# Expert rows fetched four tiles ahead, and the first tile's scatter targets made inside the attention

## The chip, the cores and the metric

The kernel runs on one core of a Trainium2 chip. The metric is the device time of one launch in microseconds (us), the median of several runs. The engines are called as in the profile: PE (matrix products), PEld (its weight loads), DVE (vector), ACT (scalar functions), POOL (general purpose, issues indirect DMAs) and SP (issues the plain DMAs). A "q" behind an engine's name means its instruction queue, so SPq is where SP's DMAs are issued.

## The reference, cut to what matters

A 64 x 64 image of 256 channels passes four residual layers; the change concerns the last step of the last one, a mixture of experts over N = 4096 tokens with 8 experts, of which each token takes its two best:

```python
def _L3_ffn_ref(x, Wg, bg, W1, b1, W2, b2):
    xf = x.reshape(-1, D)
    gate_logits = xf @ Wg + bg
    top_w, top_i = jax.lax.top_k(gate_logits, TOP_K)
    top_w = jax.nn.softmax(top_w, axis=-1)
    w_dense = jnp.sum(jax.nn.one_hot(top_i, E, dtype=xf.dtype) * top_w[..., None], axis=1)
    out = jnp.zeros_like(xf)
    for e in range(E):
        h = jax.nn.gelu(xf @ W1[e] + b1[e], approximate=False)
        out = out + w_dense[:, e:e + 1] * (h @ W2[e] + b2[e])
    return out.reshape(B, L, D)
# ...
t = t + _L3_attn_ref(_ln_t(t), ...)   # full attention over all 4096 tokens
t = t + _L3_ffn_ref(_ln_t(t), ...)    # D = 256, hidden 1024, E = 8, TOP_K = 2
```

## The kernel before, in words

Lines are those of the kernel before, as the profile names them.

**Routing.** A token is not run through all experts. `route_parts` handles a block of 512 tokens (NBLK = 8 blocks, TPB = 4 groups of 128 tokens each): it normalises the tokens, finds the two best experts and their weights, works out for each token a row in a table `xs` in HBM where the rows of one expert stand together, and scatters the normalised tokens there with indirect DMAs from POOL (L2117, 8 a block, 1 us of POOL each). A row carries C + 4 = 260 numbers: the token, its own number, its two weights and its first expert.

**Tiles.** The table is worked off in tiles of MT = 256 rows. `full_table` makes the list of the first FULL = 20 tiles (called A, with `exA`, `inA`, `offA`) when seven of the eight blocks are routed: those tiles are full already and do not depend on the last block. `tile_table` makes the list of the rest (B) after the last block. 36 tiles run; three more stand in a conditional part that was not executed.

**The expert loop** (`expert_tiles`) works on tile i in these steps:
- `load` (`expert_load`, L2219) has SP read two table entries into registers and issue three DMAs: the rows f_x (L2229, 260 KB), the first weights f_w1 (L2231, 1028 KB) and the second weights f_w2 (L2233, 1152 KB). It runs `ahead` = 2 tiles before the tile is used. The rows have ahead + 3 = 5 buffers; each of the two weights has two, and every third tile uses a third one, lent from the pool `keep`. So SP waits before f_w2 until the tile three before has been finished with.
- `turn` (`expert_turn`, L2238) transposes the rows on PE (L2241); DVE copies them out as f_xT (L2242).
- `first` forms f_h_ps = f_w1 x f_xT, eight groups of 128 hidden units (PE, L152) in three PSUM buffers; ACT takes them out with the gelu (L2303).
- `where` (L2320 to L2333) works out, from f_x and the tables, where each row's output goes (f_at) and its weight (f_wgt): nine DVE operations on 128 x 2 numbers. The first, f_first (L2325), needs the rows of f_x; f_at (L2331) is what the output's scatter reads its targets from. Each result has four buffers, so f_at of tile k takes the place of that of tile k - 4 and waits until the scatter of tile k - 4 has ended.
- `sides` has POOL form four differences of the second weights (f_wt, L2344).
- `second` with `seven` (L2347 on) forms the product with f_w2 in seven instead of eight parts: DVE makes four sums of f_h (f_hs, L2351 to L2354), PE the products f_ya and f_yb, ACT a copy (L2368), DVE the sums (L2369 to L2373) and the bias add, called Y in the text (f_y, L2379). ACT scales Y by the token's weight (L2386), and POOL scatters it in two halves to the table `ys` (L2387).

The loop issues for tile i: load(i + 2), first(i), sides(i), a step of the last block's routing, turn(i + 1), where(i + 1), second(i - 1), a further step. So the second product lags one tile.

**Around the start.** The attention of this layer (`attn3`, L2485 on) goes over 8 blocks of queries and, in each, over 16 pairs of key groups. While it computes its last block, it routes the block before last, then builds table A and loads tile 0 (at pair j = TPB + 5 = 9) and turns its rows (at j = NPAIR - 2 = 14) into f_xT. The last block's attention output is finished (`finish`: PE a_q_ps, DVE f_r L2707 and t L2708) between the parts of tile 0's first product, and its routing is spread over the first tiles as six `steps`: the scatters of its rows to xs fall in tile 2's iteration, tile_table in tile 3's.

**What sets the order.** PE's and POOL's order in the attention, and PE's in the expert loop until the six steps are done, is the order in which the code is written. DVE's, ACT's and SP's order there is chosen by a scheduler from the dependences[...]. SP's row fetch for a tile waits for all scatters to xs that were issued before it in the program.

Of the kernel before, what the change touches and what calls it, by code (L numbers as in the profile page):

```python
# [10 lines left out]
F32 = mybir.dt.float32  # L11
BF16 = mybir.dt.bfloat16
I32 = mybir.dt.int32
# [6 lines left out]
P = 128  # L20
C = 256
# [71 lines left out]
class Net:  # L93
# [30 lines left out]
    def weights(self, pool, names):  # L124

        for i, name in enumerate(names):
            src = self.A[name].rearrange("(k p) n -> p k n", p=P)
            w = pool.tile(list(src.shape), F32, tag=name, name=name)
            eng = self.nc.sync if i % 2 == 0 else self.nc.scalar
            eng.dma_start(out=w, in_=src)  # L130
            self.w[name] = w

    def rows(self, pool, first, last):

        lo, hi = PR[first].start, PR[last].stop
# [2083 lines left out]
    def expert_load(self, S, tab, j, x, w1, w2, rows_first):  # L2219
        nc, A, L = self.nc, self.A, S["L"]  # L2220
        why = "worked out from counts of tokens"
        e = nc.values_load(tab[0:1, 0, j : j + 1], engines=[mybir.EngineType.SP], min_val=0, max_val=(NE - 1) * P,
                           skip_runtime_bounds_check_because=why)
        row = nc.values_load(tab[0:1, 1, j : j + 1], engines=[mybir.EngineType.SP], min_val=0, max_val=NE * N - MT,
                             skip_runtime_bounds_check_because=why)
        src = self.xs[bass.ds(row, MT), :].rearrange("(i p) c -> p i c", p=P)
        x = x()
        if rows_first:
            nc.sync.dma_start(out=x, in_=src)  # L2229
# [3 lines left out]
        nc.sync.dma_start(out=w2, in_=A[f"f{L}_w2"][bass.ds(e, P), :])  # L2233
        if not rows_first:
            nc.sync.dma_start(out=x, in_=src)
        return x, w1, w2

    def expert_turn(self, x, p, xT):  # L2238
        for k in range(2):
# [29 lines left out]
    def expert_tiles(self, S, order, wp, ps, steps, early, pre, written):  # L2269
        nc, A = self.nc, self.A  # L2270
        L = S["L"]
        tiles = range(len(order))
        of = lambda i, nm: S[order[i][0]][nm]
# [4 lines left out]
        def load(i):  # L2278
            if pre and i == 0:
                return pre["tile"]  # L2280
# [3 lines left out]
            return self.expert_load(  # L2284
                S, of(i, "tab"), order[i][1],
                lambda: wp.tile([P, NI, CX], F32, tag="x", name="f_x", bufs=ahead + 3),
                lambda: pool.tile([P, 2 * hidden + KH], F32, tag="w1", name="f_w1", **kw),
                lambda: pool.tile([P, KH * C + C], F32, tag="w2", name="f_w2", **kw),
                i > 0,
            )  # L2290

        def turn(x):
            p = ps.tile([P, 2, MT], F32, tag="x", name="f_x_ps", bufs=1 if early else 2)
            return self.expert_turn(x, p, wp.tile([P, 2, MT], F32, tag="xT", name="f_xT", bufs=3))
# [23 lines left out]
            return h  # L2318

        def where(i, x):  # L2320

            tl = lambda tag, dt=F32: wp.tile([P, NI], dt, tag=tag, name="f_" + tag, bufs=4)
            first, second, to, wgt, at = tl("first"), tl("second"), tl("to"), tl("wgt"), tl("at", I32)
            op, j = nc.vector, order[i][1]
            op.tensor_scalar(first, x[:, :, C + 3], of(i, "ex")[:, j : j + 1], None, ALU.is_equal)  # L2325
            op.tensor_scalar(second, first, -1.0, 1.0, ALU.mult, ALU.add)
            op.tensor_tensor(wgt, second, x[:, :, C + 2], ALU.mult)
            op.tensor_scalar(second, second, float(N), None, ALU.mult)
            op.tensor_tensor(to, x[:, :, C], second, ALU.add)
            op.tensor_tensor(to, to, of(i, "in")[:, j, :], ALU.mult)  # L2330
            op.tensor_tensor(at, to, of(i, "off")[:, j, :], ALU.add)  # L2331
            op.tensor_tensor(first, first, x[:, :, C + 1], ALU.mult)
            op.tensor_tensor(wgt, wgt, first, ALU.add)  # L2333
            return at, wgt

        def sides(w2):

# [61 lines left out]
        ld = {i: load(i) for i in tiles[:ahead]}  # L2399
        if pre:  # L2400
            for f in pre["ahead"][:1]:
                f()
            xT = pre["xT"]
        else:
            xT = turn(ld[tiles[0]][0])
        to = where(tiles[0], ld[tiles[0]][0])
        done = None
        for i in tiles:
            if i + ahead <= tiles[-1]:
                ld[i + ahead] = load(i + ahead)  # L2410
            x, w1, w2 = ld.pop(i)
            h = first(xT, w1, (pre["ahead"][1:] if i == 0 else ()) if steps else None)
            now = (i, h, w2, sides(w2)) + to
            step()
            if i < tiles[-1]:
                xT = turn(ld[i + 1][0])
                to = where(i + 1, ld[i + 1][0])
            if done is not None:
                second(*done)
                step()  # L2420
            done = now
# [61 lines left out]
    def attn3(self, t, S):  # L2483
# [6 lines left out]
        with (  # L2490
# [28 lines left out]
            if True:  # L2519
# [181 lines left out]
                def finish(b, i):  # L2701
                    o = bank()[:, : C + 1]
                    at = oTs[b].rearrange("p m h n -> p m (h n)")[:, :, i * P : (i + 1) * P]
                    self.mm(o, [(at[:, kt, :], wvp[:, kt, :]) for kt in range(2)])
                    ti = b * TPB + i
                    r = S["r"][:, ti : ti + 1]
                    nc.vector.reciprocal(r, o[:, C : C + 1])  # L2707
                    nc.vector.scalar_tensor_tensor(t[:, ti, :], o[:, :C], r, t[:, ti, :], ALU.mult, ALU.add)  # L2708
# [41 lines left out]
                with tc.manual_schedule(engines={ET.PE, ET.Pool}):  # L2750
                    steps = iter(())
                    for g in range(first, G + LAG):
                        if g < G:
                            scores(g)
                        values(g - LAG)
                        if g + 3 < G:
                            fetch(g + 3)
                        b, j = divmod(g - LAG, NPAIR)
                        if b > 0:
                            if j < TPB:  # L2760
                                finish(b - 1, j)
                            elif j == TPB:
                                steps = route((b - 1) * TPB, TPB)
                            elif j % 2 == 0 or b == NBLK - 1:
                                next(steps, None)
                            if b == NBLK - 1 and j == TPB + 5:
                                self.full_table(S, keep, bank)
                                one = lambda shape, tag: keep.tile([P] + shape, F32, tag=tag, name="f_" + tag, bufs=1)
                                tile = self.expert_load(S, S["A"]["tab"], 0, lambda: one([NI, CX], "x"), lambda: one([16 * P + 8], "w1"),
                                                        lambda: one([9 * C], "w2"), True)  # L2770
# [5 lines left out]
            self.experts(  # L2776
                S, [go] * 5 + [lambda: self.tile_table(S, keep, bank, True)],
                {"pool": keep, "tile": tile, "xT": xT, "ahead": [lambda i=i: finish(NBLK - 1, i) for i in range(TPB)]},
            )

    def limits3(self, S, pool):
# [252 lines left out]
```

## Time and profile before

| what | us |
|---|---|
| median of 3 runs | 3458.88 (3456.22 to 3459.38) |
| the profiled execution | 3404.69 |
| its span, first to last instruction | 3402.80 |
| PE busy in the span | 3095.0 (91%) |
| DVE busy | 2299.0 (68%) |
| POOL busy | 1460.9 (43%) |
| granted TensorE clock, mean | 0.958 of full |

Where the stages of interest lie in that span:

| stretch of the span, us | what runs | PE busy, us |
|---|---|---|
| 2700 to 2824 | attention, last block of queries | 123.57 of 124.00 |
| 2826 to 2848 | end of the attention, tile 0 | 17.26 of 22.00 |
| 2848 to 2877.5 | tiles 1 and 2 | 29.50 of 29.50 |
| 2891.5 to 2917.5 | tile 4 | 16.09 of 26.00 |
| 2931 to 3337 | steady run of expert tiles | 400.76 of 406.00 |
| 3337 to 3402.8 | last tile, outputs | 42.82 of 65.80 |

How to read the profile's lines: a line of the timeline has the start in us, the duration in us, the engine, the line of code, the operation, out<-in by the program's names, shape, and how many equal instructions were joined (x8). In brackets at its end stands how long the engine was idle before it, and what ended the wait: "<-DMA f_x<-xs" is the landing of that transfer. A line of the waits names engine, tile and line that waited, what it waited for, then us in total, how many times, and the longest. The profiled execution is a single one, and shorter than the median of the timed runs; differences worked out on it are carried over to the median.

### The profile page before, as it was taken

How to read it: one execution, taken by the hardware profiler on the slowest of the kernel's cores; microseconds unless marked ns; L12 is line 12 of the kernel's file. 1: busy time of each engine (PE TensorE's matmuls, PEld its weight loads, DVE VectorE, ACT ScalarE, POOL GpSimd, SP SyncE). 2: the span in 40 equal slices, each digit the busy share in tenths (PEclk: the TensorE clock that was granted, in tenths of full speed). 3: DMA queues.
4: the chain of work that ended last, by engine and by line, in shares of the span. 5: the costliest groups of instructions: out<-in, count | busy, mean ns of one | idle time of the engine just before them, and what ended most of it. 6: DMA issues, size and time to landing. Idle time of an engine off the chain costs nothing.

```text
span 3402.8 us, 66193 instructions
## 1 busy us (share of the span) xinstructions
PE 3095.0 (91%) x25774; PEld 2314.3 (68%) x25774; DVE 2299.0 (68%) x5331; ACT 1329.1 (39%) x2552; POOL 1460.9 (43%) x1318
## 2 busy tenths in 40 slices
PE   6789999999977899797969789999999999899997
PEld 3343444344435888766857567888888888789996
DVE  8885677577764777787855576777777776555552
ACT  4444343434425666343633352322222223333331
POOL 2028787878842555433444353000000013555552
PEclk9889999999988999898979899999999999999998
DMA  1145555521134122200158553223332224555554
GB/s 72 42 109 147 159 153 156 155 66 52 46 107 127 57 75 75 58 1 2 54 186 262 190 212 118 90 96 100 100 99 100 81 95 165 184 201 208 203 204 176
DMA packets 241688, 407.01 MB, mean 120 GB/s; under 512 B 78353, under 2 KB 152850, under 8 KB 231890
## 3 DMA queue, kind: packets, MB, share of 16 engines
q1 hardware_dynamic: 212002, 344.40, 31.7%
q0 software_dynamic: 13056, 35.93, 2.8%
q10 hardware_dynamic: 16304, 22.31, 2.0%
q8 instruction: 207, 3.39, 0.4%
q14 instruction: 119, 0.97, 0.1%
HBM read 287.07 MB, written 111.30 MB: 117 GB/s over the span
## 4 chain that ended last, share of the span: by engine, by line
PE 41%; DVE 8%; DMA 5%; issue 4%; ACT 3%; POOL 3%; SPq 0%; POOLq 0%; DVEq 0%; ACTq 0%
PE a_sa_ps L2653 6%; PE f_h_ps L152 6%; PE a_oa_ps L2692 3%; PE a_ob_ps L2692 3%; DMA ys<-f_y,f_at 3%; PE a_oc_ps L2692 3%; PE a_sb_ps L2653 3%; PE f_ya_ps L152 3%; PE l_acc_ps L1160 2%; PE f_yb_ps L152 2%; POOL ys L2387 2%; PE a_od_ps L2692 1%; PE a_q_ps L152 1%; PE a_sc_ps L2653 1%; PE a_qkv_ps L152 1%
## 5 line engine op out<-in xcount | busy, mean ns | idle before, releaser
L776 ACT COPY l_sc<-l_s 128x384 f32<-128x384 f32 (+1 forms) x632 | 304.0, 532 | 452.3 <-PE l_s L769 446.2
L781 DVE TENSOR_TENSOR l_sm<-l_s,mask 128x256 f32<-128x256 f32 (+2 forms) x628 | 308.1, 551 | 90.4 <-PE l_s L769 89.2
L152 PE MATMUL f_h_ps<-f_xT,f_w 128*128 128x256 f32 x1440 | 342.2, 388 | 29.1 <-ACT f_h L2303 19.0
L2117 POOL DMA_INDIRECT xs<-f_room,f_to x64 | 64.3, 1005 | 641.9 <-DVE a_e L2640 474.9
L152 PEld LDWEIGHTS f_h_ps<-f_xT,f_w 128*128 128x128 f32 x1440 | 262.7, 192 | 92.3 <-ACT f_h L2303 42.2
L769 PE MATMUL l_s<-l_q,l_k 32*128 32x256 f32 (+3 forms) x2944 | 270.5, 453 | 0.0
L2672 ACT ACTIVATE a_e<-a_e 128x512 f32<-128x512 f32 x256 | 156.2, 630 | 245.2 <-DVE a_e L2642 240.9
L786 POOL TENSOR_TENSOR l_sm<-l_sc,mask 128x768 f32<-128x768 f32 (+1 forms) x116 | 202.5, 1754 | 87.8 <-ACT l_sc L776 87.7
L2303 ACT ACTIVATE f_h<-f_h_ps,f_w 128x256 f32<-128x256 f32 x360 | 164.8, 470 | 178.7 <-PE f_h_ps L152 178.5
L1156 DVE TENSOR_TENSOR l_pr<-l_vk,l_w_ps 128x1280 f32<-128x1280 f32 x128 | 186.6, 1482 | 54.2 <-PE l_acc_ps L1160 35.0
L769 PEld LDWEIGHTS l_s<-l_q,l_k 32*128 32x128 f32 x2944 | 132.4, 183 | 115.2 <-issue 67.5
L2387 POOL DMA_INDIRECT ys<-f_y,f_at x144 | 147.8, 1027 | 146.2 <-ACT f_y L2386 115.9
L1160 PE MATMUL l_acc_ps<-ident,l_pr 128*128 128x128 f32 x1600 | 197.9, 278 | 6.5 <-POOL l_pr L1151 6.2
L1160 PEld LDWEIGHTS l_acc_ps<-ident,l_pr 128*128 128x128 f32 x1600 | 184.5, 144 | 13.3 <-POOL l_pr L1151 8.2
L790 POOL TENSOR_TENSOR l_sm<-l_sc,mask 128x256 f32<-128x256 f32 (+1 forms) x220 | 185.1, 869 | 15.3 <-ACT l_sc L776 14.4
L2344 POOL TENSOR_TENSOR f_wt<-f_w 128x512 f32<-128x512 f32 x72 | 90.1, 1272 | 225.0 <-PE f_ya_ps L152 201.1
L2653 PE MATMUL a_sa_ps<-a_q,a_kt 128*128 128x256 f32 x512 | 156.2, 387 | 15.6 <-DVE a_u L2658 14.7
L2657 ACT COPY a_u<-a_sa_ps 128x256 f32<-128x256 f32 x128 | 47.6, 372 | 293.7 <-PE a_sa_ps L2653 293.6
L2653 PE MATMUL a_sa_ps<-a_qt,a_kt 128*128 128x256 f32 x512 | 153.6, 382 | 0.0
L815 PE MATMUL l_b_ps<-l_sm,l_v 128*32 128x256 f32 (+2 forms) x2176 | 153.5, 372 | 0.0
L786 POOL TENSOR_TENSOR l_sm<-l_sc,mask_c 128x768 f32<-128x768 f32 (+1 forms) x64 | 122.3, 1929 | 36.5 <-ACT l_sc L776 36.0
L2692 PE MATMUL a_ob_ps<-a_et,a_vs 128*128 128x256 f32 x512 | 132.2, 381 | 0.0
(590 smaller groups left out, 7272.4 us busy)
## 6 DMA issues: line engine op xcount, KB each, us to landing
a_kt<-a_kd SPq DMA_DIRECT2D x128, 512.0 KB
f_w<-in_f_w SPq DMA_DIRECT2D x36, 1152.0 KB
f_w<-in_f_w SPq DMA_DIRECT2D x36, 1028.0 KB
xs<-zero SPq DMA_DIRECT2D x8, 4160.0 KB
l_vk<-vt SPq DMA_DIRECT2D x180, 128.0 KB
f_x<-xs SPq DMA_DIRECT2D x72, 260.0 KB
f_w<-in_f_w SPq DMA_DIRECT2D x36, 384.0 KB
l_rcp<-l_recd SPq DMA_DIRECT2D x48, 256.0 KB
```

What stands on the lines that cost most here:

```text
L152: self.nc.tensor.matmul(out, lhsT, rhs, start=(i == 0), stop=(i == len(pairs) - 1))
L769: nc.tensor.matmul(s[pair, j][:, at : at + m, :], key(hp), qs[hp], start=(z == 0), stop=(z == len(pieces) - 1))
L776: nc.scalar.copy(sc[:, j], s[1, j])
L781: nc.vector.tensor_tensor(to(pair, j, kind, at), pick(s[pair, j], kind, which), mask, ALU.mult)
L786: nc.gpsimd.tensor_tensor(out[:, :, at, :], of[:, :, which, :], bc(mask, 1, 2), ALU.mult)
L790: nc.gpsimd.tensor_tensor(to(1, j, kind, at), pick(sc[:, j], kind, which), mask, ALU.mult)
L1156: nc.vector.tensor_tensor(pr, vk, bc(held["w"][:, j, dy], 3, D), ALU.mult)
L1160: nc.tensor.matmul(acc[:, m, j, :], pf[:, dx, m * P : (m + 1) * P], self.ident, is_transpose=True, start=(j == 0 and dy == 0 and dx == 0 a ...
L2303: nc.scalar.activation(h[:, m, :], p[:, m % 2, :], AF.Gelu, bias=w1[:, 2 * hidden + m : 2 * hidden + m + 1])
L2387: nc.gpsimd.indirect_dma_start(out=self.ys_parts[(i % 4) * NI + k], in_=y[:, k, :], in_offset=None, out_offset=bass.IndirectOffsetOnAxis(a ...
L2653: mm = lambda out, i, right: nc.tensor.matmul(out, A[i], right, start=True, stop=True)
L2692: nc.tensor.matmul(out, vs[:, j, i, :], right, start=(j == 0 and side != 1), stop=(j == NPAIR - 1 and side != 0))
```

## The change

`expert_load` is cut into `expert_at` (one table entry into a register), `expert_rows` (the rows' DMA) and `expert_weights` (the two weights' DMAs), and `where` becomes `expert_where`, so that each can be called by itself. In the loop of the last layer, the rows of tile i + 4 and the weights of tile i + 2 are now asked for in iteration i (both were i + 2); the rows have 7 buffers instead of 5. With that, the rows of tiles up to 6 are asked for ahead of the last block's scatters; it was up to tile 4. Tile 0's nine operations of `where` are now written inside the attention, at pair 14, behind the transposition of its rows, into buffers of their own. The expert loop of the layer before has the same distances as it had.

```diff
+    def expert_at(self, tab, k, j, most):
+        return self.nc.values_load(tab[0:1, k, j : j + 1], engines=[mybir.EngineType.SP], min_val=0, max_val=most,
+                                   skip_runtime_bounds_check_because="worked out from counts of tokens")
+
+    def expert_rows(self, tab, j, x):
+        row = self.expert_at(tab, 1, j, NE * N - MT)
+        self.nc.sync.dma_start(out=x, in_=self.xs[bass.ds(row, MT), :].rearrange("(i p) c -> p i c", p=P))
+        return x
+
+    def expert_weights(self, L, tab, j, w1, w2):
+        nc, A = self.nc, self.A
+        e = self.expert_at(tab, 0, j, (NE - 1) * P)
         w1 = w1()
         nc.sync.dma_start(out=w1, in_=A[f"f{L}_w1"][bass.ds(e, P), :])
         w2 = w2()
         nc.sync.dma_start(out=w2, in_=A[f"f{L}_w2"][bass.ds(e, P), :])
...
+    def expert_where(self, T, j, x, tl):
+        first, second, to, wgt, at = tl("first"), tl("second"), tl("to"), tl("wgt"), tl("at", I32)
...
         ahead = 3 if L == 2 else 2 if pre or not early else 1
+        ahead_x = ahead + 2 if pre else ahead
...
+            return self.expert_rows(*tab(i), wp.tile([P, NI, CX], F32, tag="x", name="f_x", bufs=ahead_x + 3))
...
         def where(i, x):
             tl = lambda tag, dt=F32: wp.tile([P, NI], dt, tag=tag, name="f_" + tag, bufs=4)
+            return self.expert_where(S[order[i][0]], order[i][1], x, tl)
...
-        to = where(tiles[0], ld[tiles[0]][0])
+            xT, to = pre["xT"], pre["to"]
...
         for i in tiles:
+            if i + ahead_x <= tiles[-1]:
+                xs[i + ahead_x] = rows(i + ahead_x)
             if i + ahead <= tiles[-1]:
-                ld[i + ahead] = load(i + ahead)
-            x, w1, w2 = ld.pop(i)
+                ws[i + ahead] = weights(i + ahead)
+            w1, w2 = ws.pop(i)
...
             if i < tiles[-1]:
-                xT = turn(ld[i + 1][0])
-                to = where(i + 1, ld[i + 1][0])
+                xT = turn(xs[i + 1])
+                to = where(i + 1, xs[i + 1])
...
                             if b == NBLK - 1 and j == NPAIR - 2:
-                                xT = self.expert_turn(tile[0], bank().rearrange("p (k n) -> p k n", k=2), one([2, MT], "xT"))
+                                pre["xT"] = self.expert_turn(pre["x"], bank().rearrange("p (k n) -> p k n", k=2), one([2, MT], "xT"))
+                                tl = lambda tag, dt=F32: keep.tile([P, NI], dt, tag="e" + tag, name="f_" + tag, bufs=1)
+                                pre["to"] = self.expert_where(S["A"], 0, pre["x"], tl)
```

More of the change, by code (lines that the diff above doesn't have):

```diff
@@ L2217, in tile_table @@
             nc.vector.scalar_tensor_tensor(part, self.nth[:, : k * NI], float(2 * N), part, ALU.add, ALU.mult)
[L2219 to L2229, printed above, removed]
+    def expert_at(self, tab, k, j, most):
[8 more added lines that the diff above has]
+        e = self.expert_at(tab, 0, j, (NE - 1) * P)
         w1 = w1()
@@ L2233, in expert_load @@
         nc.sync.dma_start(out=w2, in_=A[f"f{L}_w2"][bass.ds(e, P), :])
-        if not rows_first:
-            nc.sync.dma_start(out=x, in_=src)
-        return x, w1, w2
+        return w1, w2
+    def expert_where(self, T, j, x, tl):
+        first, second, to, wgt, at = tl("first"), tl("second"), tl("to"), tl("wgt"), tl("at", I32)
+        op = self.nc.vector
+        op.tensor_scalar(first, x[:, :, C + 3], T["ex"][:, j : j + 1], None, ALU.is_equal)
+        op.tensor_scalar(second, first, -1.0, 1.0, ALU.mult, ALU.add)
+        op.tensor_tensor(wgt, second, x[:, :, C + 2], ALU.mult)
+        op.tensor_scalar(second, second, float(N), None, ALU.mult)
+        op.tensor_tensor(to, x[:, :, C], second, ALU.add)
+        op.tensor_tensor(to, to, T["in"][:, j, :], ALU.mult)
+        op.tensor_tensor(at, to, T["off"][:, j, :], ALU.add)
+        op.tensor_tensor(first, first, x[:, :, C + 1], ALU.mult)
+        op.tensor_tensor(wgt, wgt, first, ALU.add)
+        return at, wgt
     def expert_turn(self, x, p, xT):
@@ L2272, in expert_tiles @@
         tiles = range(len(order))
-        of = lambda i, nm: S[order[i][0]][nm]
+        tab = lambda i: (S[order[i][0]]["tab"], order[i][1])
         hidden = 256 if L == 2 else 1024
@@ L2276, in expert_tiles, with rows, weights @@
         ahead = 3 if L == 2 else 2 if pre or not early else 1
-        def load(i):
+        ahead_x = ahead + 2 if pre else ahead
+        def rows(i):
             if pre and i == 0:
-                return pre["tile"]
+                return pre["x"]
+            return self.expert_rows(*tab(i), wp.tile([P, NI, CX], F32, tag="x", name="f_x", bufs=ahead_x + 3))
+        def weights(i):
+            if pre and i == 0:
+                return pre["w"]
             lent = pre and i % 3 == 0
@@ L2283, in load @@
             kw = dict(bufs=1) if lent else dict(bufs=2) if early else {}
-            return self.expert_load(
-                S, of(i, "tab"), order[i][1],
-                lambda: wp.tile([P, NI, CX], F32, tag="x", name="f_x", bufs=ahead + 3),
+            return self.expert_weights(
+                L, *tab(i),
                 lambda: pool.tile([P, 2 * hidden + KH], F32, tag="w1", name="f_w1", **kw),
                 lambda: pool.tile([P, KH * C + C], F32, tag="w2", name="f_w2", **kw),
-                i > 0,
             )
@@ L2322, in where @@
             tl = lambda tag, dt=F32: wp.tile([P, NI], dt, tag=tag, name="f_" + tag, bufs=4)
[L2323 to L2334, printed above, removed]
+            return self.expert_where(S[order[i][0]], order[i][1], x, tl)
         def sides(w2):
@@ L2398, in expert_tiles @@
         nc.scalar.activation(wp.tile([P, 1], F32, tag="g", name="f_gelu", bufs=1), self.one, AF.Gelu)
-        ld = {i: load(i) for i in tiles[:ahead]}
+        xs, ws = {}, {}
+        for i in tiles[:ahead_x]:
+            if pre or i > 0:
+                xs[i] = rows(i)
+            if i < ahead:
+                ws[i] = weights(i)
+            if i not in xs:
+                xs[i] = rows(i)
         if pre:
-            for f in pre["ahead"][:1]:
-                f()
-            xT = pre["xT"]
-        else:
-            xT = turn(ld[tiles[0]][0])
-        to = where(tiles[0], ld[tiles[0]][0])
+            pre["ahead"][0]()
+            xT, to = pre["xT"], pre["to"]
+        else:
+            xT = turn(xs[tiles[0]])
+            to = where(tiles[0], xs[tiles[0]])
         done = None
         for i in tiles:
+            if i + ahead_x <= tiles[-1]:
+                xs[i + ahead_x] = rows(i + ahead_x)
             if i + ahead <= tiles[-1]:
-                ld[i + ahead] = load(i + ahead)
-            x, w1, w2 = ld.pop(i)
+                ws[i + ahead] = weights(i + ahead)
+            w1, w2 = ws.pop(i)
+            xs.pop(i)
             h = first(xT, w1, (pre["ahead"][1:] if i == 0 else ()) if steps else None)
@@ L2768, in attn3 @@
                                 one = lambda shape, tag: keep.tile([P] + shape, F32, tag=tag, name="f_" + tag, bufs=1)
-                                tile = self.expert_load(S, S["A"]["tab"], 0, lambda: one([NI, CX], "x"), lambda: one([16 * P + 8], "w1"),
-                                                        lambda: one([9 * C], "w2"), True)
+                                tab = S["A"]["tab"], 0
+                                pre = {"pool": keep, "x": self.expert_rows(*tab, one([NI, CX], "x")),
+                                       "w": self.expert_weights(3, *tab, lambda: one([16 * P + 8], "w1"), lambda: one([9 * C], "w2"))}
                             if b == NBLK - 1 and j == NPAIR - 2:
-                                xT = self.expert_turn(tile[0], bank().rearrange("p (k n) -> p k n", k=2), one([2, MT], "xT"))
+                                pre["xT"] = self.expert_turn(pre["x"], bank().rearrange("p (k n) -> p k n", k=2), one([2, MT], "xT"))
+                                tl = lambda tag, dt=F32: keep.tile([P, NI], dt, tag="e" + tag, name="f_" + tag, bufs=1)
+                                pre["to"] = self.expert_where(S["A"], 0, pre["x"], tl)
             left.close()
@@ L2777, in attn3 @@
                 S, [go] * 5 + [lambda: self.tile_table(S, keep, bank, True)],
-                {"pool": keep, "tile": tile, "xT": xT, "ahead": [lambda i=i: finish(NBLK - 1, i) for i in range(TPB)]},
+                {**pre, "ahead": [lambda i=i: finish(NBLK - 1, i) for i in range(TPB)]},
             )
```

## The prediction, as put on record before the changed kernel ran

> **What bounds the kernel now.** I read the page first (shares of the engines, then the chain that ended last), then the windows of the last stage, then its waits, then the timelines of DVE, PE, POOL and SP around the stalls.
>
> ```profile
> PE 3095.0 (91%) x25774; PEld 2314.3 (68%) x25774; DVE 2299.0 (68%) x5331; ACT 1329.1 (39%) x2552; POOL 1460.9 (43%) x1318
> ...
> PE 41%; DVE 8%; DMA 5%; issue 4%; ACT 3%; POOL 3%; SPq 0%; POOLq 0%; DVEq 0%; ACTq 0%
> ```
>
> PE is the bound of the whole, so a change pays only where PE stands still. The windows of the last stage (columns: width of the window, then busy us and instructions of PE, PEld, DVE, ACT, POOL, granted clock, DMA share, GB/s):
>
> ```profile
> 2826.00:2848.00 22.00, 17.26 (x75) 14.07 (x74) 17.41 (x59) 8.08 (x14) 10.10 (x8) 0.92 0.62 240
> ...
> 2891.50:2917.50 26.00, 16.09 (x95) 14.16 (x94) 10.71 (x52) 4.63 (x11) 10.70 (x11) 0.80 0.50 177
> ...
> 2931.00:3337.00 406.00, 400.76 (x2688) 365.57 (x2688) 221.74 (x577) 140.41 (x324) 223.00 (x177) 1.00 0.53 195
> ```
>
> The long third row is the steady run of expert tiles: PE idles 5.2 of 406 us. What can be won lies in the two short rows, which hold one stall each:
>
> ```profile
> 2830.91 1.13 DVE L2326 TENSOR_SCALAR f_second<-f_first 128x2 f32<-128x2 f32 x1
> ...
> 2835.09 1.11 PE L152 MATMUL a_q_ps<-a_wvp,a_oT 128*128 128x257 f32 x4 [1.99 <-DVE t L2708]
> 2836.04 3.48 PE L152 MATMUL f_h_ps<-f_xT,f_w 128*128 128x256 f32 x8
> ```
>
> ```profile
> 2900.09 0.59 DVE L2325 TENSOR_SCALAR f_first<-f_x,f_exA 128x2 f32<-128x2 f32 x1 [10.23 <-DMA f_x<-xs]
> ...
> 2906.86 3.78 PE L152 MATMUL f_h_ps<-f_xT,f_w 128*128 128x256 f32 x8 [9.91 <-ACT f_h L2303]
> ```
>
> In the first, tile 0's nine small operations hold DVE at 2830.65, the last block's f_r and t come late, and PE waits 1.99 us. In the second, DVE stands 10.23 us before tile 5's f_first, whose rows wait for the last block's scatters; with DVE held, tile 2's output comes late, ACT's scale of it late, the gelus behind that late, and PE waits 9.91 us. In the steady run, the waits between 2931 and 3320 (us in total, times, longest) hold the pair that matters below, and SP's own wait (2826 to 3340) the third:
>
> ```profile
> DVE f_at L2331 <- DMA ys<-f_y,f_at: 35.7, 25, 2.9
> PE f_h_ps L152 <- ACT f_h L2303: 5.2, 8, 1.8
> ```
>
> ```profile
> SPq L2233 <- DVE f_y L2379: 378.3, 33, 16.1
> ```
>
> DVE already waits before f_at for the landing of an older tile's scattered output, 1.4 us each, harmlessly.
>
> **What the Trainium skill says.** "PSUM — Partial Sum Buffer", section "Engine vs sequencer instructions": the queue of VectorE is strict FIFO; the trace agrees (10.23 us held). "SBUF — State Buffer", section "Who interferes with whom": a VectorE instruction with two SBUF inputs and a GpSimd instruction that reads SBUF exclude each other; the trace agrees, since Y's bias add (L2379) takes 0.69 us alone (2904.46) and 1.24 beside f_wt on POOL (2932.32), f_hs 0.69 and 1.25. "DMA: Bandwidth & Descriptors", section "Anatomy of one DMA — SWDGE (gpsimd) path": some 2 us are fixed, mostly until the last byte is confirmed; the trace's ys scatters took 2.4 us at best, 6.5 in the median, so the rest is queueing. "TensorE: Matmul & The Clock Gate", section "What's actually happening": half clock after an idle window of about 3.4 us; here eight f_h products took 3.48 us instead of 1.89 after an idle of only 1.99, and 3.78 after 9.91, so the measurement decides.
>
> **The change, part by part.** I take the order of instructions from the changed program as built, where only SP's and DVE's orders differ in the part that runs.
>
> *1. Tile 0's nine operations leave 2830.65.* The 1.99 idle goes, and with it the half-clock stretch (3.48 − 1.89 = 1.6): −3.6 at most. What is late next is tile 1's set on the same engine and a_q's own chain; I take −2.5, bounds −3.7 and 0.
>
> *2. They go into the attention.* In the built order tile 0's f_first stands on DVE between L2641 and L2642 of a pair, which is 2808.01 on the clock of before. It reads rows that SP only issues at 2811.76 (behind block 6's scatters, which POOL issues until 2810.1). A row fetch took 2.8 us (2897.30 to 2900.09), so DVE stands from 2808.0 to 2814.5. Behind it are L2642 (0.34) and L2643 (0.68), which free the score banks at 2815.7; PE wants the next scores at 2810.97. In 2700 to 2824 PE is busy 123.57 of 124 us, so nothing hides it: a stall of 4.75, and 1.6 of half clock, together +6.4 (bounds +4 and +7, if the clock stays or the wait shortens).
>
> *3. Rows four tiles ahead.* SP's two extra fetches (260 KB each; x3 and x4, 0.9 us of SP each) go where SP waits long anyway (378 us in all): nothing; without that cover 2 × 0.9. x5 and x6 now lie ahead of the scatters. The first fetch behind them is x7, and on DVE tile 7's f_first stands where tile 5's stood, before tile 2's output. It waits for the same landing: the 10.23 moves from tile 5 to tile 7, and tile 4's 25.95 us (2891.58 to 2917.53, against 13.62) stays. Gain 0; bounds −12.3 (25.95 − 13.62, all gone) and +1. To escape, rows would have to land by 2890, before POOL has issued the scatters (2895.6).
>
> *4. The nine operations of the steady run.* Their rows being there earlier, DVE's order is another one. Before, per tile: f_hs, f_xT, f_hs, ..., f_at(i+2), then the sums of output i−1 and its bias add Y. f_at has four buffers: f_at(k) waits for the landing of scatter(k−4), here a tile and a half old. After: Y(i), five of tile i+4's operations, f_hs, **f_at(i+4)**, then f_hs, f_xT, f_hs, f_hs, the sums, Y(i+1). Now f_at(i+4) waits for scatter(i): of the output that DVE has just finished. Queued behind it are f_xT, which PE's next tile needs, and Y(i+1). That closes a loop: Y, ACT scale, two scatters on POOL, landing, f_at, the rest, next Y.
>
> Its length. From Y's end to the landing: where Y was late before, so that POOL was free of f_wt, Y ended at 2949.75 and its scatters
>
> ```profile
> 2950.57 0.99 POOL L2387 DMA_INDIRECT ys<-f_y,f_at  x1 [1.36 <-ACT f_y L2386]
> 2951.86 1.12 POOL L2387 DMA_INDIRECT ys<-f_y,f_at  x1 [0.30 <-ACT f_h L2303]
> ```
>
> landed by 2958.5: 8.7. Five late ones gave 8.4 to 9.4; the weights that the same Y releases on SP (2.4 MB) lie before them. I take 8.6. From f_at to Y's end: f_at 0.1, f_hs 0.61, f_xT 0.6, f_hs 0.6 and 0.6, small ones 0.5, sums 1.9, Y 0.69 (spacings at 2925 to 2933): 5.6 alone. POOL's four f_wt operations (2930.51 to 2936.04, 5.5 us) fall into it and stretch the three f_hs and Y by 0.55 each: 7.7 to 7.8. The loop is 8.6 + 7.7 = 16.3 (bounds 8.4 + 5.6 = 14.0 and 9.4 + 8.2 = 17.6). PE's work of a tile is 13.62, so the loop decides. Y(3) began at 2918.70 and Y(32) at 3320.96 before: 402.26 / 29 = 13.87 each, and f_at(7) to f_at(35) are 29 turns. 29 × (16.3 − 13.87) = +70.5 (bounds +4 and +108).
>
> **Sum.** +70.5 + 6.4 − 2.5 + 0 = +74.4. The profiled execution took 3404.69 us (span 3402.80 and 1.89 around it); it would become 3479.1. It lies 54.2 below the median of the runs, and I carry the difference over: 3458.88 + 74.4 = 3533.3.
>
> **Rivals.** *The loop is shorter.* If f_wt falls elsewhere or the scatters come back sooner, it is 14.0 to 15.0, say 14.5: 29 × 0.63 = +18.3, with +3.9 from the rest 3481. For it: f_wt starts when PE ends a tile's second product, and a slower tile moves that. Against: f_wt is 5.5 of 16 us and must lie somewhere. *The loop fits under PE, and the change is not slower.* Mechanism: scatters that return as fast as the best seen. Y's end to the second scatter's issue was 2949.75 to 2952.98, 3.2; with a flight of 2.4 that is 5.6, and 5.6 + 7.7 = 13.3 is under 13.62. It decides from a landing 5.9 us after Y's end. Then PE's small gaps go: 29 × (13.87 − 13.62) = −7.2, with −2.5 and +6.4 3455.6: no difference; if the wait in the attention also cost nothing, 3449.2, faster. Against: the burst of weights starts from the same Y, and no flight in the steady run was near 2.4. *The row wait goes as well* while the loop stays (the place of tile 7's f_first being harmless): −12.3, 3521; I count it within my forecast.
>
> **Chances.** Forecast (loop of 15.0 to 17.6) 0.77; short loop 0.16; loop under PE 0.07, of which 0.04 without a difference and 0.03 faster. A difference under 0.2%, 6.9 us, is what a measurement here cannot tell from none. So faster 0.03, same 0.04, slower 0.93. My forecast's own range is 29 × 1.13 + 3.9 = +37 to 29 × 3.73 + 3.9 = +112, 3496 to 3571; to leave out no more than 2 in 10 I reach into the short loop, to 3480, and leave out the rest below.
>
> **What would show it.** In the profile after: f_at behind DMA ys some 29 times, 5 to 8 us each (before at most 2.9); starts of Y 16.3 apart; PE idle before f_h behind ACT's gelu by about 2.5 us a tile; DVE 6.5 us before f_first in the attention and PE idle 4.75 after it; a wait of some 10 us before f_first still in tile 4; no PE idle near 2835. I am wrong if Y's starts lie 13.6 apart (the loop has slack), or if the row wait has gone.

## The result and the profile after

The changed kernel takes 3560.99 us (median of 6 runs, 3550.98 to 3567.60), the kernel before 3458.24 in the same comparison: a ratio of 1.0296 (95% interval 1.0279 to 1.0314), +102.8 us. Forecast were +74.4 us and 3533.3, range 3480 to 3571.

The profiled execution of the changed kernel took 3567.60 us, its span is 3565.7. That is 162.9 more than the span of before, but 55.6 of these lie ahead of the third attention, in layers that the change does not touch: the one profiled execution of before went through them faster than every later one. So stages are compared from the first score product of this attention. The views of the tile a_sa_ps give its first and last start (the two numbers ahead of the semicolon; the first fence is of before, the second of after):

```profile
L2653 PEld LDWEIGHTS a_sa_ps<-a_q,a_kt x512: 186/190/337, 1953.1 to 2819.2; 128*128 128x128 f32 x171
```

```profile
L2667 PEld LDWEIGHTS a_sa_ps<-a_q,a_kt x512: 186/190/338, 2008.7 to 2886.1; 128*128 128x128 f32 x171
```

With the starts of Y (the bias add, L2379 before, L2384 after) from the timelines of DVE, the stages are:

| stage | before, us | after, us | difference |
|---|---|---|---|
| attention, first to last a_sa | 866.1 | 877.4 | +11.3 |
| last a_sa to Y(0) | 43.95 | 45.14 | +1.2 |
| Y(0) to Y(3), with the row wait | 55.55 | 58.08 | +2.5 |
| Y(3) to Y(32), 29 turns | 402.26 (13.87 each) | 494.73 (17.06 each) | +92.5 |
| Y(32) to the end | 81.84 | 81.65 | −0.2 |
| sum | | | +107.3 |

The sum is that of the two profiled executions; the medians differ by 102.8. Most of the loss, 92.5 us, is in the steady run of expert tiles. The page of after, its first part and the chain that ended last:

```profile
PE 3169.3 (89%) x25774; PEld 2363.8 (66%) x25774; DVE 2337.8 (66%) x5331; ACT 1326.5 (37%) x2552; POOL 1464.0 (41%) x1318
...
PE 37%; DVE 12%; DMA 8%; issue 5%; ACT 3%; POOL 3%; another core or an unknown queue 1%; SPq 0%; DVEq 0%; POOLq 0%; ACTq 0%
PE a_sa_ps L2667 6%; DMA ys<-f_y,f_at 5%; PE f_h_ps L152 3%; PE a_oa_ps L2706 3%; PE a_ob_ps L2706 3%; PE a_oc_ps L2706 3%; PE l_acc_ps L1160 3%; PE a_sb_ps L2667 3%; POOL ys L2392 1%; DVE l_pr L1156 1%; PE a_od_ps L2706 1%; PE a_q_ps L152 1%; PE a_sc_ps L2667 1%; PE f_ya_ps L152 1%; PE a_qkv_ps L152 1%
```

The number of instructions is the same on every engine. PE's share of the chain fell from 41 to 37%, DVE's and DMA's rose from 8 and 5 to 12 and 8; the scatters ys are now the chain's second item. The waits between 2989 and 3484, the 29 turns (us in total, times, longest), and the windows of nearly the same stretch (width, then busy us and instructions of PE, PEld, DVE, ACT, POOL, clock, DMA share, GB/s):

```profile
DVE f_at L2246 <- DMA ys<-f_y,f_at: 199.4, 29, 8.0
...
PE f_h_ps L152 <- ACT f_h L2320: 58.2, 21, 3.2
```

```profile
2990.00:3484.00 494.00, 427.76 (x2662) 381.07 (x2661) 256.50 (x574) 135.61 (x319) 225.05 (x174) 0.94 0.44 162
```

29 waits of f_at, 6.9 us each, where there had been 25 of 1.4; PE idles 66 of 494 us, and its clock is 0.94. One turn of the loop, in lines picked from the timelines of DVE and POOL:

```profile
3145.17 0.69 DVE L2384 TENSOR_TENSOR f_y<-f_y,f_w 128x512 f32<-128x512 f32 x1
3146.68 0.98 POOL L2392 DMA_INDIRECT ys<-f_y,f_at  x1 [3.14 <-ACT f_y L2391]
3147.97 1.12 POOL L2392 DMA_INDIRECT ys<-f_y,f_at  x1 [0.30 <-ACT f_h L2320]
3154.89 0.16 DVE L2246 TENSOR_TENSOR f_at<-f_to,f_offA 128x2 int32<-128x2 f32 x1 [6.64 <-DMA ys<-f_y,f_at]
3156.17 1.60 DVE L2357 TENSOR_TENSOR f_hs<-f_hs,f_h 128x512 f32<-128x512 f32 x1
3159.44 1.23 DVE L2241 TENSOR_SCALAR f_second<-f_first 128x2 f32<-128x2 f32 x1
3162.28 0.69 DVE L2384 TENSOR_TENSOR f_y<-f_y,f_w 128x512 f32<-128x512 f32 x1
```

Y ends at 3145.86, f_at starts at 3154.89: 9.03 us, called the return. The next Y ends at 3162.97: 8.08 us, called the tail. Over all 29 turns the return is 9.55 (8.73 to 11.41) and the tail 7.50 (5.88 to 8.68). In the attention, the timelines of DVE and PE:

```profile
2874.91 0.23 DVE L2240 TENSOR_SCALAR f_first<-f_x,f_exA 128x2 f32<-128x2 f32 x1 [6.50 <-DMA f_x<-xs]
...
2876.12 0.92 PE L2667 MATMUL a_sa_ps<-a_q,a_kt 128*128 128x256 f32 x2 [4.70 <-DVE a_e L2657]
```

DVE stood 6.50 us before tile 0's f_first and PE 4.70 after it; the two products that then took 0.92 instead of 0.59 show the half clock.

### The profile page after: what moved, and what is told of

Read it like the earlier page. It is cut to its first block, busy times and chain, and to the rows that moved or that the text cites. A ratio compares the mean times of both kernels' runs of the same rounds, so it can differ in the third digit from the quotient of the medians.

```text
span 3565.7 us, 66192 instructions
## 1 busy us (share of the span) xinstructions
PE 3169.3 (89%) x25774; PEld 2363.8 (66%) x25774; DVE 2337.8 (66%) x5331; ACT 1326.5 (37%) x2552; POOL 1464.0 (41%) x1318
## 4 chain that ended last, share of the span: by engine, by line
PE 37%; DVE 12%; DMA 8%; issue 5%; ACT 3%; POOL 3%; another core or an unknown queue 1%; SPq 0%; DVEq 0%; POOLq 0%; ACTq 0%
PE a_sa_ps L2667 6%; DMA ys<-f_y,f_at 5%; PE f_h_ps L152 3%; PE a_oa_ps L2706 3%; PE a_ob_ps L2706 3%; PE a_oc_ps L2706 3%; PE l_acc_ps L1160 3%; PE a_sb_ps L2667 3%; POOL ys L2392 1%; DVE l_pr L1156 1%; PE a_od_ps L2706 1%; PE a_q_ps L152 1%; PE a_sc_ps L2667 1%; PE f_ya_ps L152 1%; PE a_qkv_ps L152 1%
## 5 line engine op out<-in xcount | busy, mean ns | idle before, releaser
L152 PE MATMUL f_h_ps<-f_xT,f_w 128*128 128x256 f32 x1440 | 372.6, 411 | 86.7 <-ACT f_h L2320 64.9
L152 PEld LDWEIGHTS f_h_ps<-f_xT,f_w 128*128 128x128 f32 x1440 | 280.4, 204 | 161.1 <-ACT f_h L2320 83.5
L781 DVE TENSOR_TENSOR l_sm<-l_s,mask 128x256 f32<-128x256 f32 (+2 forms) x628 | 307.8, 550 | 92.5 <-PE l_s L769 91.4
L2349 POOL TENSOR_TENSOR f_wt<-f_w 128x512 f32<-128x512 f32 x72 | 99.8, 1404 | 284.7 <-PE f_ya_ps L152 252.6
L2667 PE MATMUL a_sb_ps<-a_qt,a_kt 128*128 128x256 f32 x512 | 132.2, 381 | 0.0
```

The lines of the kernel that those rows point to most:

```text
L152: self.nc.tensor.matmul(out, lhsT, rhs, start=(i == 0), stop=(i == len(pairs) - 1))
L781: nc.vector.tensor_tensor(to(pair, j, kind, at), pick(s[pair, j], kind, which), mask, ALU.mult)
L2667: mm = lambda out, i, right: nc.tensor.matmul(out, A[i], right, start=True, stop=True)
```

## The experiments

Theory: f_at(k) takes the buffer of f_at(k − 4), and its new place on DVE is soon behind Y(k − 4), ahead of most of the turn's work, so each turn waits for the return of the scatter that it has just begun (a closed loop, 92.5 us); the stall in the attention is a second, small loss; the row wait only moves to another tile. Rivals: the move into the attention is what costs; or the rows' transfers slow the others.

**1. The loop opened.** Eight buffers instead of four for the small tiles of `where`; DVE's order then has f_at before the sums again, as before.

```diff
-            tl = lambda tag, dt=F32: wp.tile([P, NI], dt, tag=tag, name="f_" + tag, bufs=4)
+            tl = lambda tag, dt=F32: wp.tile([P, NI], dt, tag=tag, name="f_" + tag, bufs=8 if pre else 4)
```

> The changed kernel with eight instead of four buffers for the small tiles of where, nothing else; f_at(k) then waits for scatter(k-8). Theory (a closed loop Y - scatter - landing - f_at - Y of 17.06 us a tile, because f_at(k) takes the place of f_at(k-4)): the waits of f_at behind DMA ys go from 206 us to near 0, Y starts 13.6 to 13.9 apart, and 29 x (17.06 - 13.7) = 97 us go: about 3464 us, 3455 to 3470. Rival (the rows' transfers, two tiles earlier and in more buffers, slow the scatters or the weights): the time stays above 3540. Rival (half of it is the half clock after PE's idle, which would have another cause): 3500 to 3530.

Measured: 3454.21 us against 3453.22 of before, ratio 1.0003 (0.9995 to 1.0011). f_at waits for no transfer any more, and Y starts 13.61 to 13.62 apart. The windows of the steady run:

```profile
2973.00:3367.00 394.00, 394.00 (x2666) 362.07 (x2665) 214.81 (x560) 139.43 (x319) 221.32 (x174) 1.00 0.56 203
```

PE is busy 394.00 of 394.00 us and at full clock, with the same transfers as in the changed kernel. So the whole loss of the steady run, 29 × (17.06 − 13.62) = 100 us, hangs on the four buffers, and neither the rows' transfers nor a clock of its own has a part in it. The edit took away the wait and the early place of f_at at once; this run does not tell them apart. My expected 3464 was 10 us too high: the kernel before was itself 5 us faster in this comparison (3453.22 for 3458.24), and 13.7 us a turn for 13.62 makes 2 to 3.

**2 and 3. Either half of the change alone.** Tile 0's operations back in the expert loop; and the reverse, these operations in the attention with rows two ahead.

```diff
# 2
-                                tl = lambda tag, dt=F32: keep.tile([P, NI], dt, tag="e" + tag, name="f_" + tag, bufs=1)
-                                pre["to"] = self.expert_where(S["A"], 0, pre["x"], tl)
...
-            xT, to = pre["xT"], pre["to"]
+            xT = pre["xT"]
         else:
             xT = turn(xs[tiles[0]])
-            to = where(tiles[0], xs[tiles[0]])
+        to = where(tiles[0], xs[tiles[0]])
# 3
-        ahead_x = ahead + 2 if pre else ahead
+        ahead_x = ahead
```

> The changed kernel with tile 0's nine operations put back into the expert loop; rows four tiles ahead stay, four buffers stay. Theory: the wait of 6.5 us on DVE and of 4.7 us on PE in the attention goes, the idle of 2 us near the end of the attention comes back, the loop stays: 3561 - 6.6 + (0 to 3.6) = 3554 to 3558 us, with some 200 us of waits of f_at. Rival (the move into the attention is what costs): about 3462 us.

> The other half alone: tile 0's nine operations in the attention, rows two tiles ahead as before. Theory: 3458.2 + 6.6 (the stall in the attention) - (0 to 3.6) = 3461 to 3465 us; f_at waits as before (about 36 us, at most 3). Rival (the move is what costs): above 3520 us. Second rival (it pays, as the end of the attention is freed): 3455 us.

Measured: 3554.02 us, ratio 1.0292 (1.0274 to 1.0310), for the rows alone, and 3458.68 us, ratio 1.0013 (1.0004 to 1.0021), +4.5 us (1.4 to 7.3), for the move alone. f_at waits 220.2 us in the former (32 times), 39.4 in the latter (27 times, at most 2.7). The rows make the loop, the move costs its stall: in the latter DVE stood 6.12 us before f_first and PE 4.34 behind it. The first rival falls. The former gained nothing over the changed kernel (1.0296) that could be told from none, where I had expected 3 to 7 us. Its attention is 8.2 us shorter, but tile 0's f_at now takes one of the four buffers too, so f_at of tile 4 waits 7.95 us for tile 0's scatter, PE stands 7.29 us behind that, and Y(1) follows Y(0) by 24.20 us instead of 16.24.

**4. A version to repair both.** Eight buffers, tile 0's operations in the expert loop, and rows four ahead only where they can pass in front of the scatters; DVE's f_first of tile 7 then stands behind tile 3's output.

```diff
         for i in tiles:
-            if i + ahead_x <= tiles[-1]:
-                xs[i + ahead_x] = rows(i + ahead_x)
+            k = i + ahead_x
+            if pre and k > 6:
+                k = i + ahead if i + ahead > 6 else None
+            if k is not None and k <= tiles[-1]:
+                xs[k] = rows(k)
```

> A version to repair both: eight buffers, tile 0's nine operations back in the expert loop, rows four tiles ahead only up to tile 6 (those that can pass in front of the last block's scatters), from tile 7 on two ahead as before, so that f_first of tile 7 stands behind tile 4's output on DVE. Theory: tile 4 loses its wait of 10.2 us on DVE and takes 13.6 instead of 25.95 us (-12.3), the small waits of f_at go (up to -7): 3439 us, 3433 to 3447. Rival (tile 7's rows or the weights of tile 5, still behind the scatters on SP, take the place of the wait): 3450 to 3458 us.

Measured: 3441.41 us against 3453.22, ratio 0.9966 (0.9953 to 0.9978): −11.8, where I had expected −19 (3439, from 3458.24). The row wait did go (f_first waits at most 1.3 us), but Y(3) still follows Y(1) by 36.02 us, 40.26 before, where 28 would be free of stalls. PE's timeline of tile 2's second product shows what came in its place:

```profile
2939.57 0.47 PE L152 MATMUL f_ya_ps<-f_wt,f_hs 128*128 128x128 f32 x2 [0.69 <-issue]
2941.00 0.47 PE L152 MATMUL f_ya_ps<-f_wt,f_hs 128*128 128x128 f32 x2 [0.96 <-issue]
2942.41 0.37 PE L152 MATMUL f_ya_ps<-f_wt,f_hs 128*128 128x128 f32 x1 [0.94 <-issue]
...
2943.86 1.65 PE L152 MATMUL f_yb_ps<-f_w,f_hs 128*128 128x128 f32 x7 [0.85 <-issue]
```

PE pauses 0.7 to 1.0 us after every two or three products, and no semaphore that the profile shows holds it ("issue"). The same pauses stand in the changed kernel at the same product (0.25 to 1.03 us each), and in experiments 1, 2, 8 and 9 (from 0.13 us), and at or near it in 5 and 6 (0.15 to 0.5 us); the kernel before, with four or eight buffers, and the move alone do not have them. They lie in the time of the last block's scatters, after a stretch, 2930 to 2938, in which the DMA engines had been 95% busy. Their cause is open.

**5 and 6. What the loop is made of.** No weights fetched from tile 10 on (tile i uses those of tile i − 3), and no differences f_wt formed from tile 10 on (tile i uses those of tile i − 2).

```diff
# 5
...
-                ws[i + ahead] = weights(i + ahead)
+                ws[i + ahead] = old[i + ahead - 3] if pre and i + ahead > 9 else weights(i + ahead)
+                old[i + ahead] = ws[i + ahead]
# 6
...
-            now = (i, h, w2, sides(w2)) + to
+            wts[i] = wts[i - 2] if pre and i > 9 else sides(w2)
+            now = (i, h, w2, wts[i]) + to
```

> The changed kernel without the fetches of both weights from tile 10 on: tile i uses those of tile i-3 that lie in the same buffers. Left out: the right weights for those tiles. It asks what the 9.55 us from Y's end to the landing are made of. Theory (3.4 us until the second scatter has been issued, some 2.5 us of flight, the rest queueing behind the 2.4 MB that the same Y releases): the return falls to about 6 us, 6 + 7.5 = 13.5 is under PE's 13.62, and from tile 10 on Y starts 13.6 to 13.9 apart: 25 turns x 3.3 = -83, about 3470 us. Rival (the scatter's own writing takes that long): return 9 us or more, Y 17 apart, about 3555 us.

> The changed kernel without POOL's four differences f_wt from tile 10 on: tile i uses those of tile i-2. Left out: the right differences for those tiles. Theory (f_wt costs the loop twice: it stretches DVE's two-input operations between f_at and Y, and in some turns the scatter queues behind it on POOL): the return is 8.9 us in every turn (0.82 us to the first scatter, never 2.6), the tail 5.9 us, the loop 14.8 to 15.0 us: 25 turns x 2.1 = -53, about 3502 us. Rival (f_wt falls beside the loop): 3555 us. Second rival (the landing alone decides, a shorter tail only makes the wait of f_at longer): no, since the loop is closed; it would show as 17 us.

Measured: 3481.82 us, ratio 1.0066 (1.0049 to 1.0084), and 3490.95 us, ratio 1.0103 (1.0087 to 1.0118). A turn without the weights (DVE and POOL):

```profile
3195.95 1.25 DVE L2384 TENSOR_TENSOR f_y<-f_y,f_w 128x512 f32<-128x512 f32 x1
3196.60 3.08 POOL L2349 TENSOR_TENSOR f_wt<-f_w,f_wt 128x512 f32<-128x512 f32 x2
3199.85 0.99 POOL L2392 DMA_INDIRECT ys<-f_y,f_at  x1 [0.16 <-ACT f_h L2320]
3201.14 0.97 POOL L2392 DMA_INDIRECT ys<-f_y,f_at  x1 [0.30 <-issue]
3203.66 0.16 DVE L2246 TENSOR_TENSOR f_at<-f_to,f_offB 128x2 int32<-128x2 f32 x1 [2.70 <-DMA ys<-f_y,f_at]
3209.59 1.24 DVE L2384 TENSOR_TENSOR f_y<-f_y,f_w 128x512 f32<-128x512 f32 x1
```

f_at starts 1.55 us after the end of the second scatter's instruction (3202.11 to 3203.66), where it was 4.4 to 7.1, in the median 5.7, in the changed kernel: some 4 us of the return come with the weights. The DMA views show them as a queue. In the changed kernel's turn above, from 3145.00 to 3150.90, only SP's queue (q1) moves anything although the scatters are issued from 3146.68 on; from 3150.90 to 3154.50 POOL's queue (q0) moves beside it:

```profile
q1 hardware_dynamic: 187, 1.23, 61.7%
...
q1 hardware_dynamic: 355, 1.22, 85.4%
q0 software_dynamic: 96, 0.26, 18.2%
```

Without the weights the same 96 packets are the only ones from 3201.40 to 3203.30. The Trainium skill's "DMA: Bandwidth & Descriptors", section "Anatomy of one DMA — SWDGE (gpsimd) path", gives such a DMA some 2 us of fixed cost; the 2.52 us here from the start of the second scatter's instruction to f_at agree with that, so the queue, not the fixed cost, made the return long. The return is 6.46 in this turn (6.4 to 8.5 from Y(8) on), although the scatters here start behind f_wt, 2.65 us after Y's end. The loop fits under PE, which is busy 326.00 of 326.00 us from 3074 to 3400, and Y starts 13.63 apart from Y(8) to Y(32). The time is 12 us above the 3470 that I had expected; the four runs reach from 3469 to 3487. It is the prediction's rival of the loop under PE, brought about by leaving work out. And a turn without f_wt:

```profile
3195.88 0.69 DVE L2384 TENSOR_TENSOR f_y<-f_y,f_w 128x512 f32<-128x512 f32 x1
3197.39 0.97 POOL L2392 DMA_INDIRECT ys<-f_y,f_at  x1 [11.47 <-ACT f_y L2391]
3198.66 1.14 POOL L2392 DMA_INDIRECT ys<-f_y,f_at  x1 [0.30 <-issue]
3205.33 0.16 DVE L2246 TENSOR_TENSOR f_at<-f_to,f_offB 128x2 int32<-128x2 f32 x1 [6.38 <-DMA ys<-f_y,f_at]
3209.72 0.69 DVE L2384 TENSOR_TENSOR f_y<-f_y,f_w 128x512 f32<-128x512 f32 x1
```

The tail is 5.07 us (3205.33 to 3210.41) in nearly every turn, the first scatter always starts 0.82 after Y's end, and Y starts 14.26 apart (Y(8) to Y(32)). I had expected 5.9 and 14.9: f_wt costs the tail 2.4 us and not 1.6. The Trainium skill's "SBUF — State Buffer", section "Who interferes with whom", has a VectorE instruction with two SBUF inputs contend with a GpSimd instruction that reads SBUF; this run agrees, with Y at 0.69 us in each turn from Y(8) to Y(31). The rivals of both experiments fall.

**7. The kernel before with eight buffers.** The edit of experiment 1, made in the kernel before.

> The kernel before with eight instead of four buffers for the small tiles of where. Theory (before, f_at waited 25 times for the scatter of four tiles ago, and every third or fourth turn this cost PE 0.9 us: Y 14.5 instead of 13.62 apart): Y evenly 13.62 apart, 29 x (13.87 - 13.62) = -7.2: 3446 us of 3453 in the same runs. Rival (those waits are covered): no difference.

Measured: 3447.56 us against 3454.94, ratio 0.9977 (0.9969 to 0.9985), −7.9. Y starts 13.61 to 13.62 apart throughout. The small waits of f_at, at most 2.9 us, had a price already before the change, as forecast (29 × 0.25 = 7.2).

**8 and 9. Two variants.** Experiment 1 with tile 0's operations back in the expert loop (edits 1 and 2); and experiment 4 with rows three ahead up to tile 5 (`ahead + 1` for `ahead + 2`, 5 for 6).

> Rows four tiles ahead for all tiles, eight buffers, tile 0's nine operations back in the expert loop: the first experiment without the stall in the attention. Theory: the first experiment's time less 6.6 to 8, so 0.15 to 0.25% under the kernel before, about 3447 us of 3454; DVE still waits some 8 us before f_first of tile 7 in tile 4's time, and Y(3) follows Y(1) by 39 to 40 us as before. Rival (with the attention's stall gone something else of the four tiles shows): no better than before.

> The repaired version with rows three ahead up to tile 5, two ahead from tile 6 on (eight buffers, tile 0's operations in the expert loop). It asks what takes back 8 of the 12.3 us at tile 4 in the repaired version, where PE pauses for 5.2 us in tile 2's second product with no releaser shown. If the traffic of the extra rows ahead of the scatters does it, the pauses go and Y(3) follows Y(1) by 29 to 32 us: 3434 us of 3454. If not, it is as the repaired version (36 us between those Y): 3442 us. If tile 6's f_first now stands before tile 2's output: as the kernel before there (40 us), 3447 us.

Measured: 3436.75 us against 3443.90, ratio 0.9979 (0.9971 to 0.9986); and 3434.20 us, ratio 0.9971 (0.9960 to 0.9982). In the former, DVE waits 8.4 us before f_first of tile 7, and Y(3) follows Y(1) by 39.57: with rows four ahead for all, the row wait stays. This run differs from experiment 1 (1.0003) in tile 0's operations alone: the move costs 0.24%, some 8 us, where f_at does not wait. In the latter the pauses of PE are as in experiment 4, and the distance is 35.91: one set of rows less ahead of the scatters does not take them away. The 3434 us are not the expected sign that the pauses went: the kernel before was itself 10 us faster here than the 3454 that the expectation starts from.

So versions 4, 7, 8 and 9 are faster than both kernels, by 0.2 to 0.3% of the kernel before. Their intervals overlap: that the rows bring anything beyond the eight buffers (0.9966 and 0.9971 against 0.9977) is not settled by these runs.

## Why the prediction came out as it did

The direction, the loop and its place were right; the size fell short by 28 us of 103, and the loop was taken for new, which it was not.

*Step 2, the stall in the attention: right, or a little low.* Forecast were a DVE wait of 6.5 and +6.4 in all; DVE waited 6.50, PE 4.70, and the copies of the scores (a_u) ran 60.3 us behind those of before ahead of the stall and 66.94 behind it: +6.6. The other 4.7 of the attention's +11.3 came in small steps, most of 0.6 to 0.8 us, over its whole length. In all traces together, the attention took 876.4 to 877.4 us with the move (five) and 866.1 to 871.4 without it (six), 8.0 more in the mean, as experiments 1 and 8 have it; so some 3 us of the +11.3 are the scatter between executions.

*Step 3, the row wait stays: right.* Y(2) follows Y(1) by 25.86 us, 26.02 before. DVE's wait before tile 7's f_first was only 6.3 instead of 10.2; PE's pauses, 2.8 us in sum, lie ahead of it, and that they take up the rest is not shown.

*Step 1, the freed end of the attention: wrong in sign, small.* Forecast was −2.5, and the view gives +1.2 up to Y(0). The idle of 1.99 us shrank to 1.15, and its half clock went. What was late next I had named but sought in the wrong place: tile 1's f_xT, which is behind tile 2's operations on DVE, three of them stretched to 1.0 to 1.2 us while POOL works on f_wt.

```profile
2909.37 1.02 DVE L2240 TENSOR_SCALAR f_first<-f_x,f_exA 128x2 f32<-128x2 f32 x1
2910.42 1.19 DVE L2241 TENSOR_SCALAR f_second<-f_first 128x2 f32<-128x2 f32 x1
...
2911.72 1.23 DVE L2247 TENSOR_TENSOR f_first<-f_first,f_x 128x2 f32<-128x2 f32 x1
...
2913.08 0.68 DVE L2255 COPY f_xT<-f_x_ps 128x512 f32<-128x512 f32 x1
```

```profile
2913.86 8.83 PE L152 MATMUL f_h_ps<-f_xT,f_w 128*128 128x256 f32 x32 [4.21 <-issue]
```

PE waited 4.21 us before tile 1's first product (2.21 before), and the product took 8.83 instead of 7.14, with a granted clock of 0.57 from 2914 to 2918. Steps 1 and 2 together were forecast as +3.9; the move alone measured +4.5 (1.4 to 7.3), and some 8 between experiments 1 and 8.

*Step 4, the closed loop: it came; one term was mis-sized, and the kernel before misread.* The loop is 17.06 and not 16.3 us: 29 × 0.76 = 22 of the missing 28. The tail was forecast as 7.7 and is 7.50. The return was forecast as 8.6 and is 9.55. I had taken 8.6 from five late outputs of the kernel before; in the eight turns of its steady run whose first scatter starts within 1.3 us of Y's end, f_at starts 8.8 to 9.5 us after it. In the loop, POOL still worked on f_wt at Y's end in 8 of the 29 turns, the first scatter started 2.6 us after it instead of 0.8, and the return was 10.3; in the other 21 it was 9.3. My upper bound (9.4 + 8.2 = 17.6) held it.

A larger sample lay in the same trace. The prediction has f_at of the kernel before wait for a scatter "a tile and a half old". Counted through, the timelines show that from f_at(7) on, f_at(k) stood between Y(k − 4) and Y(k − 3) there as well, and waited for the scatter of the output just finished. Here f_at is that of tile 12 and the scatter that of tile 8:

```profile
2988.88 1.24 DVE L2379 TENSOR_TENSOR f_y<-f_y,f_w 128x512 f32<-128x512 f32 x1
2994.32 0.97 POOL L2387 DMA_INDIRECT ys<-f_y,f_at  x1 [0.31 <-issue]
2997.41 0.69 DVE L2354 TENSOR_TENSOR f_hs<-f_h,f_hs 128x512 f32<-128x512 f32 x1
3001.37 0.61 DVE L2331 TENSOR_TENSOR f_at<-f_to,f_offA 128x2 int32<-128x2 f32 x1 [2.60 <-DMA ys<-f_y,f_at]
3003.39 1.57 DVE L2379 TENSOR_TENSOR f_y<-f_y,f_w 128x512 f32<-128x512 f32 x1
```

Over the same 29 turns the return was 10.05 and the tail 3.83 us: together 13.87, the loop of before, 0.25 us above PE's 13.62. It was closed already, and nearly hidden, because f_at came behind all four f_hs and f_xT. In the changed kernel f_at comes behind the first f_hs only; the other three and f_xT now wait with it. With the same four buffers, the new place lengthened the tail by 3.7 us, while the return fell by 0.5: 3.2 us a turn, the 92.5.

*The rivals.* The shorter loop (14.0 to 15.0) and the loop under PE did not come; experiments 6 and 5 show how far they were: without f_wt it is 14.26, without the weights' burst it fits. "What would show it" named 5 to 8 us of wait for f_at (6.9), 4.75 of PE idle in the attention (4.70) and no idle near the old 2835, where 1.15 us remained.

## What to carry to other kernels

Fetching something earlier also moves what reads it: where a scheduler sets the order, look at what the moved operations wait for in their new place, and count the buffers of everything they write. A small tile that an indirect DMA reads is held until that DMA has landed. With four buffers its writer waited in both kernels for the scatter just issued: late in the turn this cost 0.25 us a tile, early in it 3.4. Eight buffers removed both costs. Small waits that seem harmless can be a loop that is just as long as the bound, so work out return plus tail and compare it with the bound before moving anything. Take the two turn by turn, and from turns in the state that the loop itself will be in.

## What the runs showed of the hardware that I had not expected

- A scatter of 2 × 128 rows issued by POOL let its waiting reader start 1.55 us after the end of the issuing instruction with the queues empty, and 4.4 to 7.1 us after it in the changed kernel, where SP issues 2.4 MB of weights and rows around the same Y. In one such turn none of its packets moved in the 4.2 us after the first scatter's start (experiment 5 against the changed kernel).
- A DVE operation on 128 × 2 numbers takes 0.13 to 0.23 us when POOL has no f_wt running. Beside f_wt, 58 of 101 in the changed kernel's expert tiles took over 0.5 us, most of them 1.1 to 1.26, close to one operation of POOL (1.25); one-input operations as well (f_second from f_first, 2910.42).
- PE can pause 0.13 to 1.03 us between products of one group with no releaser shown (in all eight traces here with rows fetched earlier, near the last block's scatters); the cause stayed open.
